# One load for the constants, idle products in PE's early gaps, and a list schedule made anew

## The chip, the cores and the metric

The kernel runs on one core of a Trainium2 chip. The core has five engines that each work through a queue of their own in order: TensorE (PE, with its weight loads shown apart as PEld), VectorE (DVE), ScalarE (ACT), GpSimd (POOL) and SyncE (SP, which here only issues transfers). They meet through semaphores. Data lies in HBM, in the on-chip memory SBUF with 128 partitions, and in PSUM, eight banks in which PE accumulates. The metric is the device time of one execution in microseconds. Matmul results are in 32 bits; most operands are split into a 16-bit high part and a 16-bit low part, so that products of 16-bit operands keep the accuracy of 32 bits.

## The reference

The input u has 2 sequences of 2048 rows of 512 numbers. First a state-space layer, then a feed-forward layer, each with a residual and a normalization:

```
zxbcdt = u @ W_in.T                       # 512 -> 1024 z | 1152 xBC | 8 dt
dt  = softplus(zxbcdt[..., -8:] + dt_bias)
xBC = silu(conv_b + causal convolution of xBC with conv_w, 4 taps)
x (8 heads of 128), B (64), C (64) = split(xBC);   A = -exp(A_log)
# scan over rows:  state = state * exp(dt*A) + dt * outer(x, B);   y = C . state + x * D
yg = y * silu(z);   yn = yg * rsqrt(mean(yg*yg) + 1e-5) * norm_w
x1 = layernorm(u + yn @ W_out.T)
# feed-forward, weights made ternary: clip(round(w/s), -1, 1) * s with s = mean(|w|) + 1e-8
out = layernorm(x1 + (silu(x1 @ Wup.T) * (x1 @ Wgate.T)) @ Wdown.T)     # 512 -> 2048 -> 512
```

## The kernel before

**Stages.** The 4096 rows are cut into 16 groups of 256 (g = 0 to 15), each with two chunks of 128 (c = 0, 1). `proj` loads a group's u, scales and splits it into uh and ul, and runs the projections: z steps (z00 to z12, twelve matmuls of 344 columns each) and x steps (x0 to x8, twelve matmuls of 260 columns). Each uses one of two PSUM banks called mm. After an x step ACT applies bias and the last tap (t.3) and DVE adds three taps (t.0 to t.2); then PE transposes the result (xt, xe). `steps` computes dt and the cumulative sums (cmm on PE), stores them to HBM (cst) and reads them back spread over all partitions (cr, 512 KB each, and ec, 256 KB). `scan` computes a chunk: gps, the state update (st), the part from the old state (yo), the part inside the chunk (yd0, yd1), then the gate (yg), the sum of squares (ssq on ACT), the power on POOL (pw), the scaled 16-bit copies yh and yl, their transposes by DMA (th, tl, issued by SP) and the output projection o0, o1, o2 into the bank po. The result goes to HBM (ss).

Beside this, the three feed-forward weights are read twice in 48 pieces each time, once for the mean of their absolute values and once to make them ternary, and are stored as 16-bit numbers in HBM. Then the feed-forward part runs over 8 blocks of 512 rows (b = 0 to 7). It makes the up and gate products with a scheme of seven products for eight (steps FP1 to FP7 for each of 8 pairs of column blocks, eight matmuls of 256 columns each), and the down projection (steps Fd, four for each of four chunks, eight matmuls of 512 columns each).

**The start.** `wsplit` loads a piece of W_in (wz0 to wz2, wx0 to wx8), squares and sums it on ACT, adds over partitions by a matmul with ones (the "scale products" named ...mm), takes a power on POOL, and splits the piece into hi on ACT and lo on DVE. W_out is loaded twice in eight pieces: wa0 to wa7 for the sum of squares, wb0 to wb7 for the split; the pieces go through three buffers called fraw. The small constants (conv_w, conv_b, norm_w, dt_bias, A_log, D) come by six DMAs in one step, cst0. From them come negA (ACT) and dmat (DVE, eight steps dm0 to dm7).

**What sets the order.** Nothing is executed where it is written. Each step is recorded by `op(name, engine, cost, function, r=..., w=...)` in an `Order`, with a cost in us and with what it reads and writes. `Order.run` then makes a list schedule: it moves a clock forward, and whenever an engine is free it takes the ready step with the smallest key for which buffers are free. Then it emits the steps in that order. So each engine's queue, and the buffers, follow from the plan. The key is from `TABLE` when the step's name stands there (plus the group's origin, 46 us apart for groups, 77 for blocks), and otherwise the latest start that follows from due times. A transfer of kb kilobytes ends `lat` after its issue, and not before the transfers ahead of it, plus kb*1.024/BW:

```
end = now + cost + o.lat
if o.kb:
    end = pipe = max(end, pipe) + o.kb * 1.024 / self.BW
```

The transposes th, tl and FT have no kb and a fixed latency of 3.1, outside this pipe.

Of the kernel before, what the change touches and what calls it, by code (L numbers as in the profile page):

```python
# [10 lines left out]
F32 = mybir.dt.float32  # L11
F16 = mybir.dt.float16
AF = mybir.ActivationFunctionType
# [4 lines left out]
P = 128  # L18
TG = 256
HL = 4  # L20
TW = TG + HL
NC = TG // P
NH = 8
DM = 512
# [11 lines left out]
FPERIOD = 77.0  # L36
TABLE = {
    "t13": -297.79, "gps.0": -277.84, "sz11": -277.47, "v1": -272.48, "T20": -271.52, "xs1": -269.6, "wb6hi": -267.22,
    "B110": -267.08, "pw.0": -262.45, "dm2": -261.6, "th.0": -261.59, "t00": -256.64, "xt0": -248.53, "ul": -240.2,
    "t83": -239.59, "Fa1.7": -238.36, "o0.0": -235.81, "wx2mm": -233.03, "wx2lo": -229.11, "sz12": -228.44, "Fs2":  # L40
    -227.08, "usmm": -223.21, "Fk2.5": -222.44, "wx2pw": -220.98, "yo.1": -220.16, "v0": -214.95, "t73": -214.51,
    "gm.1": -211.39, "wx3lo": -209.76, "Fe3": -204.12, "yd0.1": -201.94, "xe0": -201.56, "b120": -199.4, "T13": -195.77,
    "t11": -195.01, "wamm": -194.59, "B210": -193.1, "wx8hi": -192.63, "wz2mx": -192.53, "b121": -192.27, "t51":
    -192.08, "xt6": -191.78, "b126": -191.06, "T15": -189.11, "wx1pw": -188.03, "wa1sq": -182.91, "T26": -182.28,
    "Fc12.5": -180.1, "b122": -179.39, "wz2ld": -179.38, "nA1": -174.16, "cmm": -173.48, "m0.0": -171.92, "cwx3":
    -171.86, "sz01": -171.28, "Fn0": -169.79, "wx0rc": -169.11, "Fg0.3": -164.2, "wx3rc": -161.87, "FT1": -156.27,
    "wx0ld": -154.34, "Fa1.1": -151.06, "xe2": -137.44, "Fk3.4": -133.06, "T30": -126.62, "FP3.2": -124.82, "Fh0.4":
    -118.17, "Fc22.0": -115.44, "t81": -114.73, "yg0.1": -109.35, "FP6.1": -108.12, "s.0": -107.61, "xw1.0": -104.97,
    "Fg1.7": -103.39, "dm7": -92.68, "Fl0.5": -92.15, "Fc22.2": -91.96, "FP5.0": -89.18, "t42": -88.05, "cwu1": -86.79,
    "wx1mm": -82.55, "Fc11.7": -82.39, "wb3hi": -79.26, "wz1pw": -79.06, "Fc12.4": -77.49, "wasc": -74.98, "wx2ld":  # L50
    -73.27, "wx1lo": -73.26, "rs.0": -72.87, "xe4": -72.0, "xec0": -71.21, "Fk1.3": -69.91, "T46": -69.71, "dm5":
    -69.45, "Fg0.6": -69.17, "wa7sq": -68.1, "q_15": -65.99, "tl.0": -65.08, "z02": -64.67, "t71": -64.35, "yd0.0":
    -63.88, "FP3.5": -62.18, "wx1ld": -61.1, "Fk1.2": -60.36, "T40": -59.68, "cwu3": -59.33, "o2.0": -58.82, "T36":
    -58.76, "ct": -58.63, "xec1": -58.6, "wx3ld": -57.04, "t82": -55.05, "xt4": -54.06, "dm6": -52.61, "Fk2.1": -52.22,
    "Fn2": -51.92, "nA0": -50.17, "FP4.0": -48.22, "gm.0": -46.9, "q3": -45.74, "w.0": -45.7, "Fd22": -45.58, "ssq.1":
    -45.41, "cs0": -45.23, "sz10": -45.21, "szs1": -44.77, "Fa2.7": -44.33, "T42": -43.88, "Fp0": -43.18, "t12": -42.82,
    "wx1sq": -42.59, "wx3pw": -39.66, "Fq1": -38.62, "q0": -30.69, "yl.1": -30.62, "T32": -30.5, "btr": -30.36,
    "Fc11.1": -29.68, "Fr2": -28.22, "e": -27.23, "FP7.5": -25.97, "Fl1.6": -24.97, "stu.0": -24.6, "t43": -24.47,
    "yd1.1": -24.3, "xt7": -24.05, "FP4.3": -22.56, "Fc11.6": -22.24, "T43": -22.14, "Fh1.3": -20.69, "wa0ld": -18.29,
    "t80": -18.26, "Fa2.4": -17.2, "yh.0": -16.15, "Fo1": -16.12, "uh": -15.76, "Fg0.2": -15.72, "ss.0": -15.41,  # L60
    "Fa2.5": -15.1, "s.1": -13.47, "wb2lo": -13.38, "Fo2": -12.71, "FP6.3": -12.6, "Fl1.1": -9.71, "Fh1.4": -9.18,
    "usrc": -8.07, "wz0ld": -7.94, "Fm3": -7.2, "o1.0": -6.78, "wx0sq": -6.65, "Fr3": -6.51, "cwuNone": -6.5, "q6":
    -5.96, "sz02": -5.8, "FP6.4": -5.6, "Fh0.2": -5.49, "wz0mx": -5.31, "md0.0": -5.3, "B220": -5.22, "dm1": -5.16,
    "ce.1": -5.13, "Fd12": -3.71, "Fh0.0": -2.88, "T21": -2.69, "Fg1.0": -1.76, "wz0hi": -0.69, "wa2sq": -0.33, "Fk3.2":
    0.29, "wz2sq": 0.46, "wd0": 0.67, "Fm1": 1.82, "cst0": 1.96, "cwu2": 2.22, "Fo0": 3.08, "q_13": 3.57, "wx3hi": 5.42,
    "wx3mm": 5.59, "wz0sq": 6.25, "Fa1.3": 6.88, "z12": 7.02, "wz2pw": 8.16, "dec.1": 8.41, "x8": 8.96, "wz0lo": 9.2,
    "wb5lo": 9.62, "Fl0.6": 9.86, "wb6lo": 10.08, "Fl1.2": 10.73, "yg1.1": 11.61, "t40": 11.96, "t72": 12.08, "t22":
    12.2, "Fd31": 14.69, "th.1": 14.8, "wx1mx": 14.8, "xf": 18.69, "t03": 19.41, "FP6.7": 19.6, "Fp2": 19.85, "FP3.1":
    22.2, "FP7.2": 22.49, "T16": 22.97, "FP3.4": 23.14, "szsNone": 23.59, "Fg1.2": 23.69, "t30": 24.03, "FP1.0": 24.18,
    "wb4hi": 24.35, "t10": 24.43, "Fq3": 24.77, "Fk2.3": 25.13, "Fh2": 25.32, "Fp1": 25.36, "Fl0.2": 25.43, "Fk1.6":  # L70
    25.45, "Fl0.1": 25.6, "FS2": 25.67, "x1": 25.72, "Fa1.4": 25.75, "yg0.0": 25.76, "b124": 25.84, "xs6": 26.03,
    "Fg0.5": 26.49, "t62": 26.89, "FP4.1": 27.62, "xe5": 27.75, "Fd23": 27.76, "Fh0.5": 27.88, "b127": 28.01, "Fq2":
    28.26, "q_3": 28.65, "t41": 28.66, "wx2hi": 28.83, "t70": 29.25, "T10": 30.2, "Fd01": 30.4, "pw.1": 30.64, "Fh0.6":
    30.97, "T22": 31.42, "z11": 31.5, "FP7.4": 31.96, "wx1hi": 32.26, "wa5sq": 33.06, "cst": 33.07, "cr0": 33.42, "T23":
    34.64, "wa4sq": 35.06, "wb2hi": 35.35, "t31": 36.52, "wz2mm": 37.68, "t61": 38.61, "yo.0": 39.09, "t33": 39.11,
    "Fg0.1": 39.4, "wa4ld": 39.67, "xt3": 39.78, "sg10": 39.91, "x6": 39.94, "q_5": 40.23, "xs7": 40.3, "z00": 40.32,
    "yh.1": 40.51, "t01": 41.07, "FT0": 41.13, "FP7.6": 41.81, "Fe0": 42.43, "Fa1.0": 42.51, "x0": 42.53, "cwx2": 42.77,
    "T27": 43.0, "wa1ld": 43.01, "stu.1": 43.46, "Fl0": 43.93, "Fa3": 44.2, "Fh1.6": 44.48, "FP3.0": 44.52, "t32": 45.0,
    "q7": 45.02, "cum": 45.57, "ce.0": 45.72, "x2": 45.88, "Fs0": 46.02, "FT4": 46.06, "q2": 46.63, "B111": 46.74, "x3":
    46.97, "Fc11.3": 48.5, "Fc22.6": 48.53, "wx8rc": 49.28, "yg1.0": 50.26, "xw0.0": 50.58, "tl.1": 50.9, "sg00": 51.71,  # L80
    "wz2lo": 51.8, "Fg1.1": 51.9, "x5": 52.23, "FP1.1": 52.58, "wx8sq": 52.62, "ec0": 53.39, "q4": 53.72, "wz1hi":
    54.68, "FS5": 54.85, "wb5hi": 55.35, "FT6": 55.5, "Fk3.3": 56.42, "Fd00": 57.52, "wb0hi": 57.56, "Fl1.4": 58.54,
    "Fs1": 58.54, "Fg1.6": 58.59, "Fa2.2": 58.7, "t53": 58.93, "x7": 58.94, "Fc22.3": 59.02, "t20": 59.12, "Fd21":
    59.19, "FP5.1": 60.35, "Fc12.6": 61.25, "Fl1.5": 62.52, "Fh5": 62.65, "Fl1.7": 62.88, "Fh1": 63.05, "Fc22.7": 64.06,
    "o0.1": 64.55, "x4": 65.59, "FP1.2": 67.39, "Fl1.0": 67.51, "FP7.7": 67.66, "Fc12.3": 68.45, "FP1.3": 69.37, "T45":
    69.53, "xe7": 69.65, "Fc12.0": 70.39, "wa6ld": 70.44, "xt5": 70.48, "wb4lo": 70.84, "wa7ld": 71.47, "wz0rc": 71.82,
    "ulo": 71.83, "wz2hi": 72.09, "wz1rc": 72.17, "FT5": 72.24, "Fg0.7": 72.38, "wb7lo": 73.39, "z01": 73.95, "t63":
    74.45, "z10": 74.47, "t21": 74.62, "wz0pw": 75.3, "wz1sq": 75.49, "w.1": 75.5, "xs0": 75.63, "m0.1": 75.71, "wx0lo":
    75.9, "b123": 76.65, "wb0lo": 76.8, "Fc22.4": 77.04, "FP5.2": 77.93, "wb1hi": 78.35, "B211": 79.96, "T33": 80.19,
    "wx8mx": 80.31, "wx3mx": 80.88, "Fm0": 81.53, "dec.0": 81.55, "yl.0": 81.93, "Fd32": 83.39, "FP4.5": 84.52, "usq":  # L90
    85.12, "Fl0.0": 85.38, "Fk1.0": 87.94, "Fr0": 88.01, "Fk3.5": 88.48, "Fg1.4": 89.16, "Fh1.2": 89.27, "wa5ld": 89.3,
    "Fl1": 89.72, "Fg1.5": 89.87, "Fh0": 90.01, "Fk2.6": 90.02, "FP1.4": 90.14, "Fp3": 91.62, "wx8mm": 92.07, "cwx1":
    92.4, "Fh4": 93.92, "Fk3.6": 96.39, "t60": 96.75, "Fh0.3": 97.11, "md1.1": 97.67, "Fm2": 98.84, "Fa1.2": 99.42,
    "Fc12.1": 100.01, "FP4.4": 100.77, "wa0sq": 101.51, "FP4.2": 101.59, "FP3.7": 101.62, "rl": 101.81, "xe3": 101.89,
# [69 lines left out]
class Order:  # L164


    LAT = {"PE": 0.30, "V": 0.12, "S": 0.15, "G": 0.15, "SP": 1.4}
    BW = 190.0
    ENGINES = ("PE", "V", "S", "G", "SP")

# [831 lines left out]
```

## Time and profile before

| | us |
|---|---|
| median of 3 runs | 1417.15 (1416.4 to 1423.29) |
| profiled execution, its own time | 1419.3 |
| its span, first to last instruction | 1417.6 |
| PE busy | 1353.1 (95%) |
| DVE busy | 1146.0 (81%) |
| ACT busy | 827.6 (58%) |
| mean granted clock of PE | 0.989 |
| median from issue to landing of th | 4.1 (3.0 to 8.2) |
| same for a row load cr, 512 KB | 5.8 |

The profile is of one execution. An engine's queue is in order, so an instruction that waits holds up all that stand behind it on that engine. In lists of groups and waits, "A <- B" says that A stood idle until B was done, with the total in us, the number of times and the longest. "Landing" is when the data of a DMA have arrived. The granted clock is 1.00 or 0.50 in each stretch; a row over a longer time shows the mean.

### The profile page before, as it was taken

How to read it: one execution, taken by the hardware profiler on the slowest of the kernel's cores; microseconds unless marked ns; L12 is line 12 of the kernel's file. 1: busy time of each engine (PE TensorE's matmuls, PEld its weight loads, DVE VectorE, ACT ScalarE, POOL GpSimd, SP SyncE). 2: the span in 40 equal slices, each digit the busy share in tenths (PEclk: the TensorE clock that was granted, in tenths of full speed). 3: DMA queues.
4: the chain of work that ended last, by engine and by line, in shares of the span. 5: the costliest groups of instructions: out<-in, count | busy, mean ns of one | idle time of the engine just before them, and what ended most of it. 6: DMA issues, size and time to landing. Idle time of an engine off the chain costs nothing.

```text
span 1417.6 us, 26197 instructions
## 1 busy us (share of the span) xinstructions
PE 1353.1 (95%) x9956; PEld 961.9 (68%) x9956; DVE 1146.0 (81%) x2903; ACT 827.6 (58%) x1517; POOL 74.6 (5%) x128
## 2 busy tenths in 40 slices
PE   4889999999999999999999999999999999999998
PEld 2656666667676667667666785868687776768684
DVE  4798888887889889989999875959688786969564
ACT  6877666777676747665666462626354463536261
POOL 1000000000000000000000000001010100000000
PEclk9989999999999999999999999999999999999999
DMA  5435574455443654555458612132223222231200
GB/s 198 120 108 150 134 164 135 115 125 142 113 121 101 161 127 112 139 150 140 114 136 221 164 27 81 41 60 83 60 80 55 83 50 85 44 84 31 60 2 31
DMA packets 186975, 147.01 MB, mean 104 GB/s; under 512 B 134624, under 2 KB 143072, under 8 KB 186592
## 3 DMA queue, kind: packets, MB, share of 16 engines
q1 hardware_dynamic: 186848, 145.33, 39.6%
q8 instruction: 78, 1.28, 0.4%
q14 instruction: 49, 0.40, 0.1%
HBM read 90.63 MB, written 23.20 MB: 80 GB/s over the span
## 4 chain that ended last, share of the span: by engine, by line
PE 80%; DMA 7%; DVE 6%; ACT 6%; issue 1%; SPq 0%; POOL 0%; POOLq 0%; ACTq 0%; DVEq 0%
PE sd L858 18%; PE po L759 10%; PE mm L542 10%; PE mm L559 9%; PE mm L858 8%; PE po L936 8%; PE ms L936 8%; DMA th<-yh 4%; PE sd L739 2%; PE tr L858 2%; PE tr L574 2%; DVE acc L566 2%; PE sd L717 1%; PE sd L702 1%; ACT acc L564 1%
## 5 line engine op out<-in xcount | busy, mean ns | idle before, releaser
L566 DVE SCALAR_TENSOR_TENSOR acc<-mm,cwu,acc 128x256 f32<-128x256 f32 x432 | 202.4, 478 | 22.0 <-ACT acc L564 19.8
L559 PEld LDWEIGHTS <-wx 128*128 128x128 f16 x1728 | 168.2, 99 | 45.6 <-issue 5.6
L559 PE MATMUL mm<-uh,wx 128*128 128x260 f16 x1152 | 155.7, 278 | 4.8 <-DVE acc L566 2.2
L759 PE MATMUL po<-wo,th 128*128 128x512 f16 x512 | 123.7, 386 | 18.6 <-DMA th<-yh 18.3
L542 PE MATMUL mm<-wz,uh 128*128 128x344 f16 x768 | 130.2, 313 | 2.8 <-DVE acc L566 2.2
L564 ACT ACTIVATE acc<-mm,cb,cwu 128x256 f32<-128x256 f32 x144 | 80.1, 559 | 61.7 <-PE mm L559 59.2
L858 PEld LDWEIGHTS <-wx 128*128 128x128 f16 x1024 | 99.9, 98 | 15.8 <-issue 0.4
L858 PEld LDWEIGHTS <-xt 128*128 128x128 f16 x1024 | 100.0, 98 | 14.6
L858 PEld LDWEIGHTS <-wz 128*128 128x128 f16 x1024 | 99.9, 98 | 13.7 <-DVE wz L840 0.2
L542 PEld LDWEIGHTS <-uh 128*128 128x128 f16 x768 | 74.6, 100 | 39.1 <-issue 3.5
L936 PE MATMUL ms<-wo,cr 128*128 128x512 f16 x256 | 97.1, 379 | 0.0
L759 PEld LDWEIGHTS <-th 128*128 128x128 f16 x512 | 48.6, 99 | 71.5 <-DMA th<-yh 20.2
L936 PE MATMUL po<-wo,sz 128*128 128x512 f16 x256 | 97.1, 379 | 0.0
L936 PE MATMUL po<-wo,cr 128*128 128x512 f16 x256 | 97.1, 379 | 0.0
L936 PE MATMUL ms<-wo,sz 128*128 128x512 f16 x256 | 97.1, 379 | 0.0
L884 DVE TENSOR_TENSOR cr<-y,sz 128x512 f16<-128x512 f32 x128 | 86.1, 684 | 11.1 <-ACT sz L883 11.0
L883 ACT ACTIVATE sz<-y 128x512 f16<-128x512 f32 x128 | 79.5, 626 | 24.7 <-DVE y L882 23.8
L549 ACT ACTIVATE sz<-mm,szs 128x344 f32<-128x344 f32 (+1 forms) x96 | 51.8, 541 | 65.1 <-PE mm L542 60.4
L559 PE MATMUL mm<-ul,wx 128*128 128x260 f16 x576 | 89.5, 278 | 0.0
L936 PEld LDWEIGHTS <-sz 128*128 128x128 f16 x512 | 49.9, 98 | 56.0
L936 PEld LDWEIGHTS <-cr 128*128 128x128 f16 x512 | 50.0, 98 | 55.8
L862 ACT ACTIVATE ec<-sd 128x512 f32<-128x512 f32 x96 | 56.7, 591 | 36.8 <-PE sd L858 36.5
(198 smaller groups left out, 2815.2 us busy)
## 6 DMA issues: line engine op xcount, KB each, us to landing
cr<-cum_scratch SPq DMA_DIRECT2D x32, 512.0 KB, 5.8
uraw<-in_uT_dram SPq DMA_DIRECT2D x16, 520.0 KB, 3.7
ec<-cum_scratch SPq DMA_DIRECT2D x64, 128.0 KB, 5.0
fraw<-in_wupT_dram SPq DMA_DIRECT2D x32, 256.0 KB, 3.3
s_scratch<-s SPq DMA_DIRECT2D x32, 256.0 KB, 2.3
x<-s_scratch SPq DMA_DIRECT2D x32, 256.0 KB, 3.1
fraw<-in_wgateT_dram SPq DMA_DIRECT2D x32, 256.0 KB, 3.2
fraw<-in_wdownT_dram SPq DMA_DIRECT2D x32, 256.0 KB, 3.3
```

The costliest lines, as they stand in the source:

```text
L542: T.matmul(ps[:, :ZC], (uh, ul)[a][:, k, HL + c * P:HL + (c + 1) * P], wz4[b]()[:, j, k, :], start=(n == 0), stop=(n == 11))
L549: op(f"sz{c}{j}", "S", act(w, 1), lambda: S.activation(d["sz"][c][:, j * ZC:j * ZC + w], ps[:, :w], AF.Silu, scale=szs[:, j:j + 1]), r=[ps ...
L559: T.matmul(ps[:, :TW], wx4[a]()[:, j, k, :], (uh, ul)[b][:, k, :], start=(n == 0), stop=(n == 11))
L564: op(f"t{j}3", "S", act(TG, 2), lambda: S.activation(acc.ap, ps[:, HL:TW], AF.Identity, bias=cb[:, j:j + 1], scale=cwu[:, j, 3:4]), r=[ps, ...
L566: op(f"t{j}{k}", "V", stt(TG), lambda k=k: V.scalar_tensor_tensor(acc.ap, ps[:, 1 + k:1 + k + TG], cwu[:, j, k:k + 1], acc.ap, ALU.mult, A ...
L574: T.transpose(tr[:, c * P:(c + 1) * P], xc[:, c * P:(c + 1) * P], ident)
L759: T.matmul(po.ap, t[:, k, :], wo3[b]()[:, k, :], start=(q == 0 and k == 0), stop=(q == 2 and k == 7))
L858: T.matmul(bank_[:, fi * TG:(fi + 1) * TG], wt[:, kt, f * P:(f + 1) * P], xT[i][:, a, :, kt, :], start=(first and fi == 0 and n == 0), sto ...
L862: copy = lambda nm, t, bank_: o(nm, "S", 0.52, lambda: S.activation(t.ap, bank_.ap, AF.Copy), r=[bank_], w=[t])
L883: o(f"h{t}", "S", 0.54, lambda g_=g_, hv=hv, hh_=hh_: S.activation(hv(hh_), two(g_), AF.Copy), r=[g_], w=[(hh_[p // 2], (p, t))])
L884: o(f"l{t}", "V", tt(512), lambda g_=g_, hv=hv, hh_=hh_, hl_=hl_: V.tensor_tensor(hv(hl_), two(g_), hv(hh_), ALU.subtract), r=[g_, (hh_[p ...
L936: T.matmul(po.ap, h[qd][:, f, c * P:(c + 1) * P], wd[qd // 2][:, 4 * (qd % 2) + f, :], start=(qd == 0 and f == 0 and a == 0), stop=(qd == ...
```

## The change

Four things are changed.

1. The six constants are put side by side on the host into one array `small` of 128 x 77 numbers, loaded by one DMA (39 KB); cw, cb, nw, bias_b, alog and dsk are views of its tile.
2. 80 steps are added on PE. Each multiplies a constant tile (ones, read as 16-bit numbers) by itself four times with 256 columns, into the bank po. Nothing reads the result. They have no key from the table and no due time, so the planner takes one only when no other step is ready on PE at that moment of its clock. They are chained on one use of the bank po, which is free for the output projections only after the last of them.
3. The planner's numbers for transfers: an issue costs 0.5 in place of 0.4 us, latency is 1.7 in place of 1.4, the rate 290 in place of 190 GB/s, and the transposes now go through the pipe with 330 KB each.
4. A new table. Before, it had 624 keys, each for a step's name and the same in all groups; now it has 624 such keys with other values and 440 more that hold for group 0 or block 0 alone ("Fh1.3@0"). It changes the order on all engines.

```diff
+WARM = 80
 TABLE = {
-    "t13": -297.79, "gps.0": -277.84, "sz11": -277.47, "v1": -272.48, ...
+    "Fh1.3@0": -880.0, "xe4@0": -833.42, "xs3@0": -798.3, "Fr1@0": -749.32, ...
...
-    LAT = {"PE": 0.30, "V": 0.12, "S": 0.15, "G": 0.15, "SP": 1.4}
-    BW = 190.0
+    LAT = {"PE": 0.30, "V": 0.12, "S": 0.15, "G": 0.15, "SP": 1.7}
+    BW = 290.0
...
-        def consts():
-            nc.sync.dma_start(out=cw, in_=conv_w)
-            nc.sync.dma_start(out=cb, in_=conv_b)
-            nc.sync.dma_start(out=nw, in_=norm_w)
-            for i, a in enumerate((dt_bias, a_log, d_skip)):
-                nc.sync.dma_start(out=hb[:, i, :], in_=a.unsqueeze(0).to_broadcast([P, NH]))
-        op("cst0", "SP", 2.6, consts, w=[kc], lat=4.0)
+        op("cst0", "SP", 0.5, lambda: nc.sync.dma_start(out=cst, in_=small), w=[kc], kb=39)
...
+        warm = mk("po", [P, DM])
+        oh = ones.bitcast(F16)
+        for n in range(WARM):
+            def idle():
+                for i in range(4):
+                    T.matmul(warm[:, :P * 2], oh[:, :P], oh, start=True, stop=True)
+            op("", "PE", 4 * 0.109, idle, w=[warm], lat=0.0)
...
-            o("th", "SP", 1.3, lambda: nc.sync.dma_start_transpose(out=th.ap, in_=yh.ap), r=[yh], w=[th], lat=3.1)
+            o("th", "SP", 1.3, lambda: nc.sync.dma_start_transpose(out=th.ap, in_=yh.ap), r=[yh], w=[th], kb=330)
```

The same for tl and FT, and 0.5 for 0.4 at the other transfers. What the new order does to the first entries of SP's queue: before, u, wz2, wx0, wx2, wx1, wx3, wa0, wz0, the six constants, wa4, wa1; after, wb7, u, the constants, wz2, wb1, wa1, wx3, wx8, wx2, wx1, wz0. On PE, 15 of the new steps stand ahead of the first scale product, 33 ahead of the first z step, and all 80 ahead of the first yd product of group 0.

## The prediction

> **What bounds the kernel now.** I read the page's busy line first, then the table by stage, then who PE waited for, then the chain in order of time, and last the opening 20 us and the transposed tile on its own.
>
> ```profile
> span 1417.6 us, 26197 instructions
> PE 1353.1 (95%) x9956; PEld 961.9 (68%) x9956; DVE 1146.0 (81%) x2903; ACT 827.6 (58%) x1517; POOL 74.6 (5%) x128
> ```
>
> The table by stage: length, then busy time of PE, PEld, DVE, ACT, POOL, then PE clock, DMA share, GB/s.
>
> ```profile
> 0.00:20.00 20.00, 1.78 (x7) 1.56 (x7) 5.06 (x20) 8.67 (x12) 2.67 (x10) 1.00 0.79 283
> 20.00:100.00 80.00, 65.62 (x428) 47.00 (x429) 63.07 (x198) 65.57 (x127) 6.04 (x11) 0.87 0.36 100
> 100.00:740.00 640.00, 617.62 (x4532) 427.72 (x4530) 565.22 (x1723) 429.24 (x828) 27.32 (x47) 0.99 0.52 133
> 740.00:800.00 60.00, 56.92 (x425) 39.40 (x424) 54.75 (x150) 34.39 (x58) 3.14 (x4) 1.00 0.76 181
> 800.00:1411.00 611.00, 611.00 (x4571) 446.19 (x4569) 455.60 (x811) 289.74 (x493) 34.90 (x55) 1.00 0.24 60
> ```
>
> PE bounds it. From 800 us on it never rests, so nothing is to be won there; before that it is idle 18.2, 14.4, 22.4 and 3.1 us. Who it waited for, and the constants at the start:
>
> ```profile
> PE po L759 <- DMA th<-yh: 18.3, 9, 3.1
> PE ms L423 <- DVE sc L424: 6.0, 1, 6.0
> PE ms L423 <- ACT wx L435: 5.7, 2, 2.9
> PE sd L739 <- ACT fraw L783: 2.7, 1, 2.7
> ```
>
> In order of time, SP's issues and the two engines that stood still:
>
> ```profile
> 4.95 0.50 SPq L454 DMA_DIRECT2D cw<-in_conv_w_dram  x1
> 11.63 0.33 SPq L458 DMA_DIRECT2D hb<-in_d_skip_dram  x1
> 14.98 0.21 ACT L470 ACTIVATE negA<-hb 128x8 f32<-128x8 f32 x1 [5.19 <-DMA hb<-in_a_log_dram]
> 15.17 1.07 DVE L473 TENSOR_SCALAR dmat<-ident,hb 128x128 f32<-128x128 f32 x5 [5.37 <-DMA hb<-in_d_skip_dram]
> ```
>
> From the chain (start, length):
>
> ```profile
> 140.48 7.06 DMA th<-yh
> ...
> 810.26 3.49 PE sd L858 x32
> ```
>
> Two things to see: nine waits for the transposed y make 18.3 of the 22.4 us between 100 and 740, and six small loads keep SP's queue from 4.95 to 11.96 us while ACT and DVE both stand still for 5 us.
>
> **A ledger.** I gave each PE step its shortest start-to-start time in the trace (x 1.34 us, z 1.75, o and Fd 1.73, a pair product FP 0.87, yd 0.93, yo 1.09, st 1.02, xt 0.24) and summed over all steps: 1323.6 us of work. The span is that plus what is lost: 47.7 up to 100 us (53 us of work done by then), 35.3 from 100 to 740, 4.6 from 740 to 800, 0 to the end of the last matmul, 6.4 after it; together 1417.6. The table by stage on narrow stretches shows clock 0.50 at 30.9-37.8, 41.2-44.6, 75.3-82.1, 95.8-99.2, 522.5-525.9 and 618.0-621.4; PE was busy 19.0 us of the first four and 6.8 us of the last two, so half of that, 9.5 and 3.4 us, is inside those losses. The matmuls from 20.4 to 24.1 also run at half speed (1.85 us).
>
> **The constants.** Six issues (7.0 us of SP's queue) become one of 0.4 to 0.5 us, third in the queue instead of ninth, so what stood behind them (wo pieces, the second u tile, wz1, wx8) is issued some 6 us sooner, and the 5.2 us on ACT and 5.4 us on DVE go. PE's 6.0 us wait before the scale product at 16.45 ended on DVE's queue behind these; it is part of the 47.7. What is late next is the chain u load, square, scale product, pow, split: the changed queue puts one 256 KB load ahead of u, about 0.9 us at 283 GB/s.
>
> **The products that nobody reads.** 80 times four, shape 128x256 f16, the shape of the row with 32 in 3.49 us: 0.109 each, 34.9 us in all on PE. The order shows all 80 ahead of group 0's output projection, 15 of them ahead of the first scale product; when the last is through, 34.1 us of real work is also done. PE is in order, so they are no elastic filler: they are paid in full. The start then costs 1.1 us (ones are written at 1.07), 34.9, 1.85 for the first half-speed stretch, 2.2 for small losses that the ledger shows before as well (steps longer than their shortest by under 0.35 us), and the waits that remain, r. The trace has no such queue, so r is bounded: 0 if every wait is covered, 14.4 if PE still waits as much as it did between 20 and 100. The nearer row is 100 to 740, where waits other than for th are 4.1 us in 640; but the start is loads and splits, so I take a third of 14.4, r = 4.5. Sum 44.5 against 47.7: 3.2 us won, between 7.7 won and 6.7 lost. The early half-clock stretches go inside this sum.
>
> **The transfers in the planner.** The transposes now take a place behind the loads in the planned pipe, where before they had a fixed 3.1 us. In the trace the first chunk's th is issued 5.3 us (median) after its last yd product, and the output products that waited began 5.3 to 8.2 us after that issue (mean 6.7); one that did not wait began 3.1 after it. At 140.48 the issue came directly behind cr, ec, cr (138.06 to 140.2, 1.28 MB) and landed after 7 us. So the need from yd to o0 is 9.7 us with an undisturbed transfer (4.4 us from issue to product in group 15), and 12.0 behind the row loads. By the order, PE work between the two, for first chunks of groups 1 to 15, is 7.6 to 10.9 us before and 8.8 to 16.3 after (ten of them below 10.3); second chunks go from 9.5-12.5 to 11.3-19.5. Against 9.7 the changed order is short by 3.1 us in all; against 12.0 by 26.9, where the old order would be short by 31.2 and waited 18.3, so by that scale 15.8. Which end? The row loads follow cmm by 4.6 us and take 9 to clear; the old order has 0.9 us of work from the next group's cmm to the last yd, so th issues with 7.7 us of backlog; the new one has 6.6 (median), which leaves 2.0, a quarter of it. A quarter of the way from 3.1 to 15.8 is 6.3; in three of fourteen groups cmm comes after the scan altogether, so I take 6.0 us of waits: 12.3 won, between 2.5 and 15.2. What hides the row loads now is the older group's work ahead of the scan; should it be thinner, this comes back.
>
> **The clock.** Two of the waits (2.6 us to 522.3, 2.9 us to 617.2) are followed by the half-clock stretches, 3.4 us lost; with waits of under 1.5 us I take both as gone. The Trainium skill, "TensorE: Matmul & The Clock Gate", Part 1, has the array fall to half after an idle window of about 3.4 us; here waits of 2.6 and 2.9 were followed by it. By that rule these waits would not be the cause and the stretches would stay, 3.4 us more in the sum; by the row they go.
>
> **The new table elsewhere.** PE's spacing between two uses of a projection bank, and from x to its transposes, is as wide as before. DVE is busy 565 of 640 us there; when PE's waits shrink it comes closer to being the bound, and I add 2.0 us for waits that come next (half of the 4.1). From 740 to 800 I leave 4.6: the first FP now stands 12.5 us of PE work behind the last x step, where four 512 KB loads took about 9 us to land; 0 to 3 us either way. In the last block FP4.7 follows FP7.7 directly and must wait for a copy (ACT 0.59 and the handover, 0.9), and on DVE Fm0 (0.54) stands between Fr3 and Fe3: 1.5 us more at the end.
>
> **Sum.** 1323.6 + 44.5 + (6.0 + 13.6 + 2.0) + 4.6 + 0 + 7.9 = 1402.2, where 13.6 is 35.3 less 18.3 and 3.4. The profiled execution took 1419.3 for a span of 1417.6, so 1403.9; it lies 2.15 above the median of the three runs (1417.15), so 1401.8 is the forecast, 1.1% less.
>
> **Rivals.** *The start eats the gain:* r is 14.4 and the row loads still precede th (2.5 won, no clock): 1417.15 + 6.7 - 2.5 + 3.5 = 1425 at its worst, 1410 to 1420 with one of the two. For: the planner's 290 GB/s is more than the 224 GB/s that the trace reached at DMA share 0.95 (750 to 775). Against: 283 in the first 20 us.
> *Slower, by one mechanism:* two early wo pieces sit in two of three fraw buffers until the wo scale, so the eight loads for that scale go through one buffer, each waiting for ACT's square, with SP's in-order queue behind them; the store of the first cumulative sums stands behind the fourth. A round is 3.3 us (load) and 0.9 (square), planned; each microsecond that ACT is late per round counts four times. It turns the sign when group 0's rows come more than 16 us late, that is 4 us a round: about 1422. Against: before, ACT was 98% busy at 50-60, and here it is relieved by the stall.
> *All goes as planned:* r = 0, th short by 3.1, no new waits: 1401.8 - 4.5 - 2.9 - 2.0 = 1392.
> *The products do not raise the clock:* the order keeps them beside real work, so the stretches after 24 us could stay; 9.5 us more, 1411.
>
> **How the numbers follow.** Forecast, 1396 to 1409: 0.53. As planned or better: 0.17. Clock stays or half of the gain lost, 1410 to 1424: 0.17. Slower: 0.13. What a measurement can tell from no change is 0.5%, 7 us. Faster 0.70, same 0.17, slower 0.13. The range, 1391 to 1421, leaves out about one in ten at each side.
>
> **What would show it.** Right: no 5 us wait for constants; clock 1.00 from about 5 us on; waits of PE for th below 8 us in total; 800 to the last matmul still without idle PE. Wrong: PE waits of more than 8 us in the first 90 us beside the products; th waits above 12; idle PE in the last stage; half-clock stretches after the products.

## The result and the profile after

| | before | after |
|---|---|---|
| median (runs) | 1416.78 us (1415.33 to 1423.29, 4) | 1400.92 us (1399.6 to 1401.88, 4) |
| profiled execution, its own time | 1419.3 | 1400.29 |
| its span | 1417.6 | 1398.6 |

The ratio is 0.9879, with a 95% interval of 0.9847 to 0.9911. In a second set of runs it was 0.9863 (0.9833 to 0.9892). The forecast of 1401.8 us, 1.1% less, lies 0.9 us above the measured median.

The busy line of the page of the changed kernel:

```profile
span 1398.6 us, 26861 instructions
PE 1373.4 (98%) x10276; PEld 986.8 (71%) x10276; DVE 1141.8 (82%) x2903; ACT 858.7 (61%) x1539; POOL 85.8 (6%) x128
```

PE has 320 matmuls more, the 80 steps of four. The table by stage of the changed kernel, with columns as before (length; busy time of PE, PEld, DVE, ACT, POOL; PE clock, DMA share, GB/s):

```profile
0.00:20.00 20.00, 18.88 (x157) 15.89 (x158) 7.71 (x28) 12.61 (x20) 4.16 (x11) 1.00 0.85 301
20.00:100.00 80.00, 75.26 (x618) 59.38 (x617) 65.00 (x203) 63.55 (x123) 5.82 (x10) 1.00 0.43 123
100.00:740.00 640.00, 629.03 (x4655) 438.31 (x4653) 575.07 (x1769) 460.35 (x866) 39.44 (x49) 1.00 0.51 135
740.00:800.00 60.00, 59.09 (x440) 41.75 (x439) 51.96 (x124) 38.86 (x60) 1.10 (x2) 1.00 0.71 189
800.00:1392.00 592.00, 591.10 (x4413) 431.48 (x4411) 439.34 (x779) 283.30 (x474) 34.23 (x54) 1.00 0.22 56
```

The clock reads 1.00 from 20 to 100 us, where it was 0.87. (For the first row the reading decides nothing: what lies ahead of a trace's first record of the clock counts as full. The first row of the kernel before also reads 1.00, and its matmuls run at half speed until 24.1 us. Here the record begins at 4.0 us, at full clock: from 1.1 to 4.0 us 14 of the new matmuls run, from 4.1 to 7.0 us 29.) From 100 to 740 us PE is idle 11.0 us in place of 22.4. In the first row PE looks full, 18.88 of 20 us, but most of that is products that nobody reads. So a busy share says little here, and the ledger of the prediction (1323.6 us of PE work, and what is lost beside it) is the better measure:

| lost, us | before | forecast | after |
|---|---|---|---|
| until 53 us of work are done | 47.7 | 44.5 | 44.6 |
| from there to 740 | 35.3 | 21.6 | 19.4 |
| 740 to 800 | 4.6 | 4.6 | 3.3 |
| 800 to the last matmul, and the tail | 6.4 | 7.9 | 0.9 + 6.7 |

Who PE waited for from 100 to 740 us in the changed kernel (total us, times, longest), the first three lines:

```profile
PE po L833 <- DMA th<-yh: 4.2, 3, 1.6
PE tr L648 <- ACT xt L650: 2.0, 5, 0.7
PE mm L616 <- DVE acc L640: 1.5, 3, 1.0
```

The first line was 18.3 us in nine waits before. The transposed tile of the changed kernel, 28 issues of first and second chunks in this stretch, landed as follows (shortest, median, longest); before, it was 3.0, 4.3 and 8.2 in this stretch:

```profile
DMA to landing us min/median/max: 3.0/3.1/7.4
```

And the constants at the start of the changed kernel, in order of time:

```profile
6.83 1.66 DVE L538 TENSOR_SCALAR dmat<-ident,cst 128x128 f32<-128x128 f32 x8 [5.74 <-DMA cst<-in_small_dram]
7.60 0.19 ACT L535 ACTIVATE negA<-cst 128x8 f32<-128x8 f32 x1
```

negA comes at 7.60 us in place of 14.98. DVE's bracket still reads 5.74 us, but that is the start of the program, before which it has only its memsets to do; PE shows no wait for it.

### The profile page after: what moved, and what is told of

It is laid out like the page before. It is cut to its first block, busy times and chain, and to the rows that moved or that the text cites. A ratio compares the mean times of both kernels' runs of the same rounds, so it can differ in the third digit from the quotient of the medians.

```text
span 1398.6 us, 26861 instructions
## 1 busy us (share of the span) xinstructions
PE 1373.4 (98%) x10276; PEld 986.8 (71%) x10276; DVE 1141.8 (82%) x2903; ACT 858.7 (61%) x1539; POOL 85.8 (6%) x128
## 4 chain that ended last, share of the span: by engine, by line
PE 49%; ACT 2%; DVE 2%; DMA 1%; issue 0%; POOL 0%; POOLq 0%; ACTq 0%; DVEq 0%
PE sd L932 18%; PE ms L1010 8%; PE mm L932 8%; PE po L1010 8%; PE po L833 2%; PE tr L932 2%; PE mm L616 1%; PE mm L633 1%; DMA th<-yh 1%; PE sd L813 1%; DVE acc L640 0%; DVE cr L806 0%; ACT L743 0%; ACT L644 0%; ACT L745 0%
## 5 line engine op out<-in xcount | busy, mean ns | idle before, releaser
L640 DVE SCALAR_TENSOR_TENSOR acc<-mm,cwu,acc 128x256 f32<-128x256 f32 x432 | 198.4, 474 | 24.1 <-ACT acc L638 22.6
L633 PE MATMUL mm<-uh,wx 128*128 128x260 f16 x1152 | 152.5, 274 | 2.4 <-DVE acc L640 0.9
L638 ACT ACTIVATE acc<-mm,cst,cwu 128x256 f32<-128x256 f32 x144 | 79.1, 557 | 53.9 <-PE mm L633 51.9
L936 ACT ACTIVATE xw<-sd 128x512 f32<-128x512 f32 x63 | 37.5, 595 | 62.1 <-PE sd L932 33.3
```

The source lines that it names most:

```text
L633: T.matmul(ps[:, :TW], wx4[a]()[:, j, k, :], (uh, ul)[b][:, k, :], start=(n == 0), stop=(n == 11))
L638: op(f"t{j}3", "S", act(TG, 2), lambda: S.activation(acc.ap, ps[:, HL:TW], AF.Identity, bias=cb[:, j:j + 1], scale=cwu[:, j, 3:4]), r=[ps, ...
L640: op(f"t{j}{k}", "V", stt(TG), lambda k=k: V.scalar_tensor_tensor(acc.ap, ps[:, 1 + k:1 + k + TG], cwu[:, j, k:k + 1], acc.ap, ALU.mult, A ...
L936: copy = lambda nm, t, bank_: o(nm, "S", 0.52, lambda: S.activation(t.ap, bank_.ap, AF.Copy), r=[bank_], w=[t])
```

## The experiments

The question was which of the four parts made the 16 us, since all of them came together. The ratios are to the kernel before on the same chip.

**The products.** The steps keep their places in the plan; they only emit nothing.

```diff
             def idle():
-                for i in range(4):
-                    T.matmul(warm[:, :P * 2], oh[:, :P], oh, start=True, stop=True)
+                pass
```

> The changed kernel with its plan and every queue kept, but the 320 products left out; nothing reads them, so the output is the same. Theory (the products pay by the clock: they fill waits that would be there anyway): PE idles in their place, the start is set by loads, ACT and DVE, half-clock stretches come back before 100 us, and the time rises by 3 to 9 us, to 1404-1410. Rival (they are paid in full on an in-order queue and the clock is worth less): the first scale product runs 1 to 2 us sooner, the real work moves up, and the time falls to 1390-1400.

Measured: 1397.96 us (four runs, 1396.95 to 1398.98), ratio 0.984 (0.9822 to 0.9858). Nothing is lost without the products; the rival held. The table by stage of this run, without the products:

```profile
0.00:20.00 20.00, 6.60 (x24) 4.31 (x25) 8.56 (x30) 13.46 (x21) 3.15 (x11) 1.00 0.90 320
20.00:100.00 80.00, 64.57 (x451) 46.77 (x450) 67.07 (x209) 64.58 (x127) 5.80 (x10) 0.89 0.44 126
```

PE is idle 13.4 and 15.4 us here, and the clock is down to 0.89, and yet 41.7 us are lost at the start in place of 44.6. The products do hold the clock, but they delay what stands behind them in PE's queue: the first scale product starts at 9.07 us with them and at 7.08 without, the first z step at 17.58 and 15.62. (Not all of it is theirs: what the first scale product needs was done on ACT at 7.69 us in the changed kernel, so some 1.4 of the 2.0 us are the queue's.) The two places where this kernel is worst, from the timeline of PE without the products (start, length; the bracket is the idle time before it and what ended that):

```profile
27.93 1.89 PE L632 MATMUL mm<-uh,wx 128*128 128x260 f16 x8 [4.21 <-ACT sz L622]
63.87 1.92 PE L632 MATMUL mm<-uh,wx 128*128 128x260 f16 x8 [5.55 <-DVE acc L639]
```

Eight matmuls of an x step take 1.89 and 1.92 us here, and 1.05 in the changed kernel: half the clock.

**The one load.** Six DMAs at the place of the one, third in SP's queue; the plan is kept.

```diff
-        op("cst0", "SP", 0.5, lambda: nc.sync.dma_start(out=cst, in_=small), w=[kc], kb=39)
+        def consts():
+            nc.sync.dma_start(out=cw, in_=conv_w)
+            nc.sync.dma_start(out=cb, in_=conv_b)
+            nc.sync.dma_start(out=nw, in_=norm_w)
+            for t, a in zip((bias_b, alog, dsk), (dt_bias, a_log, d_skip)):
+                nc.sync.dma_start(out=t, in_=a.unsqueeze(0).to_broadcast([P, NH]))
+        op("cst0", "SP", 0.5, consts, w=[kc], kb=39)
```

> The changed kernel with its plan kept, but the six small loads of before in place of the one, at the same place of SP's queue. Theory (the one load is what lets the early plan hold): what stands behind it on SP is issued some 6 us later, the first weight piece among it, PE waits that much beside the products, and the time rises by 4 to 7 us, to 1405-1408. Rival (the products and the other loads hide it): 1400-1402.

Measured: 1399.08 us (1397.12 to 1400.27), ratio 0.9846 (0.9827 to 0.9866). The theory fell: six loads cost nothing that can be measured beside the products; 43.2 us are lost at the start.

**The queue's order alone.** The kernel before, with its plan; on SP the row loads of the next group (cr, ec) that stood ahead of th of the first chunk are put directly behind it.

```diff
-        for o in self.run():
+        for o in self.rows_behind(self.run()):
...
+    def rows_behind(self, out):
+        for g in range(15):
+            at = {(o.nm, o.g): i for i, o in enumerate(out)}
+            th = at["th.0", g]
+            late = [o for o in (out[at[nm, g + 1]] for nm in ("cr0", "ec0", "cr1", "ec1"))
+                    if at[o.nm, o.g] < th and min(at[s.nm, s.g] if s.nm else out.index(s) for s in o.succ) > th]
+            rest = [o for o in out if o not in late]
+            th = rest.index(out[th])
+            out = rest[:th + 1] + late + rest[th + 1:]
+        return out
```

> The kernel before with one edit of its order on SP alone: the next group's row loads (cr, ec), where they stand ahead of the first chunk's transpose th, are issued directly behind it. All other queues are as before. Theory (th is late because it queues behind 1.28 MB of row loads): PE's waits for th fall from 18.3 to under 6 us, the two half-clock stretches after 500 us go, and the time falls to 1400-1405. Rival (the transpose is slow in itself, or the row loads then come late and a new wait takes the place): waits of 12 us or more in sum, 1412-1419.

Measured: 1421.44 us against 1421.78, ratio 1.0003 (0.9987 to 1.0018). PE's longest waits from 100 to 740 us in this kernel:

```profile
PE tr L585 <- ACT xc L581: 10.7, 7, 3.3
PE mm L570 <- DVE v L558: 5.1, 4, 3.6
```

and what DVE waited for there:

```profile
DVE cr L661 <- DMA cr<-cum_scratch: 29.5, 12, 7.0
```

The waits for th are gone from the list altogether, and from issue to landing th takes (shortest, median, longest)

```profile
DMA to landing us min/median/max: 3.0/3.1/5.5
```

in place of 3.0, 4.3 and 8.2. So the reason was right: th was late because it stood behind 1.28 MB of row loads. But the rows are now late instead, as the rival had it. DVE waits 29.5 us for them (0.8 in the whole kernel before), in order; what it owes ACT and PE comes late, and PE is idle about as long as before (20.6 us from 100 to 740 in place of 22.4), under other names. To gain, both transfers would have to be early; moving the work that feeds the rows is a way to that, which no run here shows by itself.

**The table under the old picture of transfers.** The changed kernel, planned anew with the planner's old numbers; table, products and one load stay.

```diff
-    LAT = {"PE": 0.30, "V": 0.12, "S": 0.15, "G": 0.15, "SP": 1.7}
-    BW = 290.0
+    LAT = {"PE": 0.30, "V": 0.12, "S": 0.15, "G": 0.15, "SP": 1.4}
+    BW = 190.0
...
-            o("th", ..., r=[yh], w=[th], kb=330)
+            o("th", ..., r=[yh], w=[th], lat=3.1)
```

(tl and FT in the same way, and 0.4 for 0.5 at the issues.)

> The changed kernel with its table, products and one load, but the planner's transfers as before (latency 1.4, 190 GB/s, issue 0.4, transposes at a fixed 3.1 outside the pipe). The plan changes with it. Theory (modelling the transposes is what took the th waits away): waits for th of 10 to 18 us come back and the time is 1408-1418. Rival (the table's order does it): th waits under 7 us, 1399-1405.

Measured: 1434.95 us, ratio 1.0102 (1.0068 to 1.0137). Neither theory held: it is slower than the kernel before. PE's waits from 100 to 740 us:

```profile
PE mm L616 <- DVE acc L640: 6.0, 5, 3.7
PE po L833 <- ACT s L836: 5.5, 4, 2.3
PE mm L633 <- ACT sz L623: 4.1, 3, 2.3
...
PE po L833 <- DMA th<-yh: 2.7, 2, 2.5
```

th is not what is wrong here, with 2.7 us. PE loses 45.5 us in this stretch by the ledger, in place of 35.3 before: it is idle 27.2 us in place of 22.4, in many smaller waits for ACT and DVE, and 13.7 us run at half clock in place of 6.8.

**The picture of transfers under the old table.** The kernel before with the new latency, rate and place of the transposes, and nothing else.

```diff
-    LAT = {"PE": 0.30, "V": 0.12, "S": 0.15, "G": 0.15, "SP": 1.4}
-    BW = 190.0
+    LAT = {"PE": 0.30, "V": 0.12, "S": 0.15, "G": 0.15, "SP": 1.7}
+    BW = 290.0
...
-            o("th", ..., r=[yh], w=[th], lat=3.1)
+            o("th", ..., r=[yh], w=[th], kb=330)
```

> The kernel before with the planner's new picture of a transfer alone (290 GB/s, 1.7 us, transposes that queue), its old table kept, six constant loads, no products. PE work between the last yd product of a first chunk and its first output product is 7.0 to 12.6 us (median 10.1, as before), from the next group's cumulative product to that yd product 1.5 us (as before). Theory that the picture of the transfers carries the gain: th waits of PE under 9 us and the time 1402 to 1408 (0.988 to 0.993). Rival, that the table belongs to the picture it was made with, as the new table with the old picture showed (1.0102): th waits of 12 to 18 us or others in their place, 1415 to 1440 (0.998 to 1.015).

Measured: 1427.66 us, ratio 1.0061 (1.0037 to 1.0084). PE's waits from 100 to 740 us:

```profile
PE mm L559 <- DVE acc L566: 5.6, 3, 2.5
PE tr L574 <- ACT xc L570: 4.5, 3, 1.9
PE mm L542 <- DVE acc L566: 2.8, 3, 1.6
...
PE po L759 <- DMA th<-yh: 2.0, 2, 1.1
```

The rival held. This is the mirror image: the picture alone takes the waits for th from 18.3 to 2.0 us, and puts more in their place. The planner places every step by key and by what it believes to be ready. With either half changed alone, other steps are late; the likely reason is that keys found for one picture order the steps badly under another, but for no single step is this shown. The run with the new table alone also has the products and the one load, which by the other runs move the time by a few us, not by 13. And one rival is left without a run: a table searched anew, with its 440 keys more, under the old picture. So the runs show that this table needs this picture, not that the better picture was needed for a better table.

**One load in the kernel before.** Its plan and queues are kept, only the six loads become one at their old place.

```diff
-        op("cst0", "SP", 2.6, consts, w=[kc], lat=4.0)
+        op("cst0", "SP", 2.6, lambda: nc.sync.dma_start(out=cst, in_=small), w=[kc], lat=4.0)
```

> The kernel before, its plan and queues unchanged, with one load of 12.5 KB or so in the place of the six constant loads. Theory that the six issues hold up the start: SP's queue is 5.5 to 6.5 us sooner behind them, the 5 us stalls of ACT and DVE for constants go, and the start (47.7 us lost up to 100 us) wins 2 to 6 us: ratio 0.9955 to 0.9985, lost up to 100 us 42 to 46. Rival, as in the changed kernel with six loads, which took no longer: the wait of PE for the constants' users is replaced by one for the scale chain or for the loads of wz and wx, 0.999 to 1.001, lost 47 to 48.

Measured: 1417.53 us against 1420.23, ratio 0.9992 (0.9969 to 1.0015): no difference. ACT in this run:

```profile
14.38 0.21 ACT L462 ACTIVATE negA<-cst 128x8 f32<-128x8 f32 x1 [4.52 <-DMA cst<-in_small_dram]
```

The stall is 4.52 us long, where it was 5.19. So it is not the six issues that made ACT wait; the transfer is late because of its place in the queue, behind the loads of u, wz, wx and W_out. The changed kernel with six loads shows the other side: they stand third in the queue, and ACT waits for them only 1.12 us.

```profile
8.21 0.21 ACT L541 ACTIVATE negA<-cst 128x8 f32<-128x8 f32 x1 [1.12 <-DMA cst<-in_a_log_dram]
```

With one load at the old place 44.1 us are lost at the start (47.7 before), but 6.5 from 740 to 800 (4.6 before), and what is left of that is too small to show in the time.

**Neither products nor one load.** The changed kernel's table and planner with six loads and no products; and beside it, once more, without products but with one load.

> The changed kernel without products and with six constant loads in the place of the one. Theory that the one load is worth something once no products fill the stretch that it opens: 2 to 5 us more than without products and with one load, ratio 0.9855 to 0.988, and the first scale product or the first z step (7.1 and 15.6 us) later by as much. Rival, as with products: hidden behind the loads and scales of wz and wx, within 1 us, 0.983 to 0.985.

> The changed kernel without its products once more, on the chip of this set, beside the next three. Measured before: 0.984. If products cost the path about 3 us net, 0.982 to 0.986 again.

Measured: six loads 1398.85 us (1398.26 to 1403.95), ratio 0.9855 (0.9834 to 0.9876); one load 1398.51 us (1397.16 to 1403.22), 0.9859 (0.9837 to 0.9881). The two differ by 0.3 us, so the one load is worth nothing here either. The table and the picture of transfers together carry all of the gain that the change has.

**Fewer products.** If products hold the clock but delay the queue, they should stand only where PE would be idle for long. Two places qualify in the run without products: eight steps where 4.2 us were idle, eleven where 5.6 us were.

```diff
-            def idle():
+            def idle(n=n):
+                if not (35 <= n < 43 or 60 <= n < 71):
+                    return
```

> The changed kernel with 19 of its 80 products: eight in the place where PE without products was idle for 4.2 us (23.7 to 27.9) and eleven where it was idle for 5.6 us (58.3 to 63.9), each of which was followed by 6.8 us at half clock. Theory that products pay where they fill an otherwise idle stretch and keep the clock: both half-clock stretches go (3.2 us of PE work saved, 5.8 and 4.0 us busy in them, half of each 4.9 at most), span 1391 to 1393.5, ratio 0.981 to 0.983. Rival, that the waits that follow take it up again (PE's steps there wait for ACT's and DVE's work, which is no sooner): span 1394 to 1396, ratio 0.9835 to 0.985, as without products. If any product costs its length on the path: 1396 or more.

> The changed kernel with 19 products in the two places where PE would be idle for 4 to 6 us, once more. If filling those two places pays, it ends 1 to 3 us below the run without products beside it; if a wait for DVE and ACT takes the gain up, within 1 us of it.

Eleven more were tried beside them (`22 <= n < 25 or 28 <= n < 30` and `51 <= n < 57`), together with the changed kernel on the same chip:

> As the run with 19 products, with eleven more: five in the gaps of 2.2 and 1.4 us ahead of the first z step (15.6), to have the clock up by then, and six between 37 and 43. By the first theory 0.5 to 2 us less than with 19 (the matmuls from 15.6 to 20.1 ran at half clock without products, 2.2 us; the stretch from 44.0 to 47.4, 1.7 us); by the rival the same time within 0.7 us, or up to 2 us more, because products at half clock take 0.87 us each and delay the first z step.

> The changed kernel as it is, on the chip of this set, so that the others have it beside them: ratio to the kernel before 0.985 to 0.991, as measured (0.9879).

| | median us (runs) | ratio |
|---|---|---|
| changed kernel, 80 products | 1401.43 (6) | 0.9863 (0.9833 to 0.9892) |
| 19 products, same chip | 1397.66 (5) | 0.9835 (0.9801 to 0.9869) |
| 30 products, same chip | 1400.06 (5) | 0.9853 (0.9823 to 0.9883) |
| 19 products, other chip | 1395.61 (4) | 0.9833 (0.9811 to 0.9855) |
| none, that other chip | 1398.51 (5) | 0.9859 (0.9837 to 0.9881) |

With 19 products it is 3.8 us (medians) under the changed kernel on one chip and 2.9 under the kernel without products on the other. By the means the first is 3.6, with standard errors of 0.9 and 0.6 for the two, so some 2.5 either way: a gain, but just. It is the fastest kernel here. The second expectation, 1 to 3 us under the kernel without products, was met; the first, 0.981 to 0.983, was not reached, and 0.9835 lies at the edge of what its rival gave. In the timeline of PE of the second run with 19 products, the two places look like this:

```profile
27.08 1.06 PE L635 MATMUL mm<-uh,wx 128*128 128x260 f16 x8 [0.71 <-ACT sz L625]
32.59 1.07 PE L635 MATMUL mm<-uh,wx 128*128 128x260 f16 x8 [2.43 <-DVE acc L642]
62.03 1.07 PE L635 MATMUL mm<-uh,wx 128*128 128x260 f16 x8 [0.75 <-DVE acc L642]
```

Both x steps run at full clock, and part of what the first won is waited away 5 us later (2.43 us for DVE), as the rival had it. In the first run with 19 products that same wait is followed by half clock (from 33.1 us, 3.4 us long), so the clock is not held everywhere. Between 80, 30 and 0 products the differences are 1 to 3 us and the intervals overlap (80 and 0 never stood in one set of runs); that all 80 cost some 2 us against none is likely from the ledgers (42.4 and 44.6 us lost at the start against 40.6 and 41.7), but not settled. Why 30 are slower than 19 by their medians stays open; the traces, with spans of 1396.3 and 1396.6, do not help, because one is of the fastest of the five runs with 30 and the other of the slowest of the five with 19.

## Why the prediction was right

**The sum.** The span came out at 1398.6 where 1402.2 was forecast. The terms that differ: 100 to 740 us 2.2 less, 740 to 800 1.3 less, the end 0.3 less, the start 0.1 more. The other error had the opposite effect: the profiled execution was taken to lie 2.15 us above the median, as in the kernel before, but after the change it lies 0.6 below. The 0.9 us at the end is the rest of two errors of 3.6 and 2.8 us; that it is so small is luck.

**The waits for th.** Forecast 6.0 us, measured 4.2. The reason given, the row loads ahead of th on SP's queue, was shown by moving them: the waits vanished. The step "PE work from the next group's cmm to the last yd" carried the estimate, and the quarter of the way that it gave was near. (The backlog of 7.7 and 2.0 us does not follow from the figures beside it, 4.6, 9, 5.3, 0.9 and 6.6, which give 7.4 and 1.7; it stays a quarter.) What the prediction said only half of is that the rows must not pay for it. "What hides the row loads now is the older group's work ahead of the scan" is the condition that the queue's order alone broke.

**The constants.** That the stalls go was right (negA at 7.60 us). That the six issues were their cause was wrong: one load at the old place left 4.52 of 5.19 us, and six loads at the new place cost nothing. The step that failed is "what stood behind them is issued some 6 us sooner" as a reason for a gain: with one load in the kernel before, the two loads of W_out behind it are issued at 6.55 in place of 12.29 us, and the time stays the same.

**The products.** "They are paid in full" held as a sum, since r was put at 4.5 and came out at 4.6: 44.6 less 1.1, 34.9, 1.85 and 2.2. This is luck in part: r was chosen between 0 and 14.4 without a row that shows such a queue (a third of 14.4 is 4.8, not 4.5), and the first half-speed stretch, from 1.1 to 4.0 us, cost 1.4 in place of 1.85, which makes r 5.0. PE's listed waits in the first 100 us, without that for ones, sum to 4.4. And the sum hid the comparison that matters. Without the products the same queue loses 40.6 to 41.7, so the 3.1 us won at the start are the new order's, in spite of the products and not through them. The rival "the products do not raise the clock" fell: the clock is full from 4.0 us to the end of the last matmul.

**The clock after 500 us.** The two stretches of 3.4 us went, as forecast. The reason, waits of 2.6 and 2.9 us, was incomplete; see below.

**The new waits.** 2.0 us were added for waits that come next, on top of 4.1. Beside th, PE's waits from 100 to 740 us are now 6.8 (11.0 idle less 4.2), against the 6.1 forecast. DVE is busy 575 of 640 us there and is not yet the bound.

**740 us to the end.** FP4.7 behind FP7.7 cost its 0.9 (0.7 of it a listed wait, the only one after 800 us); Fm0 cost 0.3 in place of 0.6. From 740 to 800 the first pair product did not wait, and 1.3 us more were won.

**The slower rival**, the eight loads of W_out through one buffer, did not come about: the store of the first cumulative sums, behind the fourth of them, is issued at 39.45 us, where before it was at 51.27, and the first row load at 42.99 in place of 54.18.

## What to carry to other kernels

A late transfer in an in-order queue can be fixed by its place, but what is moved behind it must have a reader that is still later: look at who waits for that before counting the gain. When a plan's costs are corrected, its keys belong with them: here the new costs under the old keys made the kernel 9 us slower, the new keys under the old costs 13 us, and both together some 20 us faster. Filler work for the clock paid here only where the engine would be idle for more than a whole clock window of 3.4 us (4.2 and 5.6 us), and it is to be compared with the same queue without it, not with the old kernel.

## What was not expected of the hardware

The clock does not fall after a wait of some length; it goes by windows of fixed length, one directly after the other. The half-clock stretches of the kernel before begin at 30.9, 41.2, 75.3, 95.8, 522.5 and 618.0 us. The distances are 10.3, 34.1, 20.5, 426.7 and 95.5, which are 3, 10, 6, 125 and 28 times 3.41. Pairs of windows of the kernel before, each followed by the next:

```profile
71.90:75.30 3.40, 0.70 (x6) 0.73 (x7) 3.32 (x10) 3.40 (x10) 0.00 (x0) 1.00 0.08 27
75.30:78.70 3.40, 2.83 (x13) 1.38 (x13) 3.40 (x12) 3.37 (x6) 0.00 (x0) 0.50 0.51 146
92.40:95.80 3.40, 1.46 (x13) 0.74 (x12) 3.40 (x13) 3.19 (x7) 1.09 (x2) 1.00 0.00 0
95.80:99.20 3.40, 3.40 (x17) 2.01 (x15) 2.42 (x9) 2.27 (x6) 0.55 (x1) 0.50 0.41 76
519.10:522.50 3.40, 0.80 (x7) 0.55 (x6) 3.40 (x10) 0.86 (x3) 0.00 (x0) 0.99 1.22 130
522.50:525.90 3.40, 3.40 (x10) 1.53 (x9) 0.08 (x1) 0.20 (x1) 0.00 (x0) 0.50 0.65 162
191.40:194.80 3.40, 1.42 (x13) 1.23 (x11) 3.40 (x8) 1.06 (x3) 0.00 (x0) 1.00 1.21 177
194.80:198.20 3.40, 2.32 (x14) 1.31 (x15) 3.40 (x16) 1.16 (x3) 0.55 (x1) 1.00 1.06 172
471.20:474.60 3.40, 1.69 (x16) 1.50 (x14) 3.40 (x11) 0.92 (x2) 0.00 (x0) 1.00 1.11 283
474.60:478.00 3.40, 3.36 (x22) 2.12 (x23) 2.71 (x14) 1.54 (x4) 0.55 (x1) 1.00 0.91 241
```

The first number in each row after the length is PE's busy time in the window; the clock in the row below is the answer. Over all such windows at full clock, in the traces of all 14 runs, every one in which PE was busy under 40% was followed by half clock, and none with over 60%. From 41 to 59% both happen: 1.46 us (43%) was followed by half clock, 1.42 (42%) and 1.69 (50%) were not. So 2.6 us of waiting in one window, 0.80 us busy, is enough. The longest wait for th, 3.06 us up to 195.88, was not followed by half clock: a window's edge at 194.8 cuts it in two, and PE is busy 42 and 68% in the two windows. The other six, from 0.96 to 2.48 us, all leave PE busy 45% or more in every window that they touch. The Trainium skill, "TensorE: Matmul & The Clock Gate", Part 1, gives a window of 3413 ns that runs freely, and that agrees with the distances above. It has the clock fall after an idle window; here the window need not be wholly idle, as these rows show.

It also explains why the mean clock differs between runs of one kernel. The kernel without products has half clock at 26.8 to 33.7, 43.9 to 47.3 and 61.0 to 67.8 us in one profiled run, and in the other for 3.4 us each from 28.4, 62.5 and 734.9. The first two of these:

```profile
28.20:31.60 3.40, 2.74 (x14) 2.00 (x14) 2.72 (x16) 3.35 (x7) 0.55 (x1) 0.52 0.01 2
...
62.50:65.90 3.40, 3.28 (x17) 2.50 (x16) 3.40 (x11) 1.97 (x6) 0.00 (x0) 0.50 0.23 66
```

The waits ahead of these are nearly the same (4.21 and 5.55 us in the one, 4.21 and 4.89 in the other); the windows lie differently over them. Whether it also makes the times differ is not shown: the first of these runs, with more half clock, has the shorter span (1394.9 and 1396.3 us). In the kernel before, the two go together (1428.44 us at a mean clock of 0.988, 1413.16 at 0.993, in one set).
